# Gabor stage of a four-layer kernel: the way back over the rows for two channel groups at once, and the next group's rows forward placed ahead of it

## Chip, cores and metric

The kernel runs on one core of a Trainium2 chip. The metric is device time in microseconds, the median of three runs. A profile of one further execution is read beside it. The engines are called as the profile calls them: PE is TensorE's matmul and PEld its weight load, DVE is VectorE, ACT is ScalarE, POOL is GpSimd, and SP is SyncE, which issues the DMAs.

## The reference, cut to what matters

The program chains four layers over an image `x` of 4 x 64 x 128 x 128 float32: a Mamba layer, a Gabor layer, two convolutions with a gate, and a Mamba layer with a feed-forward part. The change touches the second layer, which computes, with `NUM, SIZE = 4, 32`:

```python
agray = x.reshape(B, a, b, C)                     # 4 x 128 x 128 x 64
rr, hh = analysis_window_r0(q, LEN, NUMBER)       # q from the image's gradients
S = rrb[d[:, :, None, None], d[None, None, :, :]]
ag = agray.reshape(B, num, size, num, size, C)
R1 = jnp.einsum('bikjlc,minjkl->bmnklc', ag.astype(jnp.complex64), S)
FT = jnp.fft.fft2(R1, axes=(3, 4))
xb = (FT.real - FT.imag).reshape(B, a, b, NB, bs)
o1 = jax.nn.relu(jnp.einsum('...bi,bio->...bo', xb, w1) + b1)
o2 = jnp.einsum('...bi,bio->...bo', o1, w2) + b2
xs = _softshrink(o2, LAMBD).reshape(B, num, num, size, size, C)
Rf = jnp.fft.fft2(xs, axes=(3, 4))
aa = Rf.real - Rf.imag
Gm = hh[ridx[:, :, None, None, :], ridx[None, None, :, :, :]]
I = jnp.einsum('bmnklc,xmynl->bxkylc', aa, Gm).reshape(B, a, b, C)
return I.reshape(B, C, a, b) + bias               # bias = x
```

So each image goes through a windowed transform over its rows and its columns, a small block-diagonal network over channels with a soft threshold, a transform back over columns and rows, and the image is added.

## The kernel before

`layer1` first computes the window (gradients over the whole image, then an iterative dual window), and builds constant matrices: `fa` and `fb` for the transforms forward over rows and columns, `ga` and `lt` for those back. Then it loops over the 4 images `b` and, in each, over 4 groups `g` of `G = 16` channels: 16 groups in all. An image is held in SBUF as `X`, with a row of the image in each partition and 128 columns by 64 channels in it. A group goes through six steps of TensorE, each of which writes PSUM tiles of 1024 elements a partition; all of them come from one ring of four (`ps`):

- Rows forward (L1041): for each channel, the weights are `X[:, :, c]` and the moving operand is `fa`, 256 columns. DVE copies the four tiles to `Z` (L1044), which has two buffers.
- Columns forward (L1052): weights from `Z`, moving operand `fb`, 128 columns. ACT copies two tiles to `O` (L1059).
- The network's first layer (L1065), 512 columns; ACT applies the relu into `O1` (L1066).
- Its second layer (L1072), 128 columns. DVE adds the bias into `xs` (L1073) and clamps it into `cl` (L1075), POOL subtracts the clamped part (L1076), which is the soft threshold. This is done in two halves, and `cl` has one buffer, so the second clamp waits for the first subtraction.
- Columns back (L1083): weights are one channel of `xs`, whose elements lie 16 floats apart; moving operand `ga`, 256 columns. ACT copies four tiles to `V` (L1086), laid out as `p i c (y l)`: real and imaginary part, channel, column.
- Rows back (L1094): for each of the 32 values of `l` two matmuls, for `i` 0 and 1, accumulate in PSUM. The weights are `lt[:, i, l]`, the moving operand is `Vl[:, i, l]`, 4 values of `y` by 16 channels, 64 columns. Channels lie 128 floats apart in it. DVE adds two tiles of 16 `l` each to `X` in place (L1101).

When an image's groups are done, SP stores `X` (L1102). `X` has two buffers and SP loads an image ahead (L1029).

The work is issued in the order in which the code states it, engine by engine, and each engine takes its own instructions in that order. Waits between engines are set by the tiles that they share. In the code below the way back of a group is therefore followed on TensorE by the rows forward of the next.

Of the kernel before, what the change touches and what calls it, by code (L numbers as in the profile page):

```python
# [10 lines left out]
F32 = mybir.dt.float32  # L11
# [6 lines left out]
P = 128  # L18
B, C, HH, WW = 4, 64, 128, 128
# [4 lines left out]
NUM, SIZE = 4, 32  # L24
# [7 lines left out]
G = 16  # L32
# [705 lines left out]
def _gradients(ctx, tc, K, x1, out):  # L738
# [9 lines left out]
    with tc.tile_pool(name="sob", bufs=2) as sp, tc.tile_pool(name="sobc", bufs=1) as sc, tc.tile_pool(  # L748
# [5 lines left out]
        for b in range(B):  # L754
            img = x1[b].rearrange("c (h r w) -> (c h) r w", h=2, w=C)
            for r0 in range(0, HH, R):
                X = sp.tile([P, R + 2, C], F32, name="X", tag="X")
                h = sp.tile([P, R + 2, C + 1], F32, name="h", tag="h")
# [205 lines left out]
@with_exitstack  # L964
def layer1(ctx, tc, K, w, x1, x2):
    nc = tc.nc
    cp = ctx.enter_context(tc.tile_pool(name="l1c", bufs=1))

    mg = cp.tile([P, 1], F32, name="mg")
    _gradients(ctx, tc, K, x1, mg)  # L970

    lm = cp.tile([P, 1], F32, name="lm")
    nc.scalar.activation(lm, mg, AF.Ln, scale=20.0 / (HH * WW))
    nscale = cp.tile([P, 1], F32, name="nscale")
    nc.scalar.activation(nscale, lm, AF.Exp, scale=0.5)
    nc.vector.tensor_scalar_mul(nscale, nscale, -math.pi / 25.0)
    amp = cp.tile([P, 1], F32, name="amp")
    nc.vector.tensor_scalar(amp, lm, 0.125, 0.25 * math.log(2.0) - 0.5 * math.log(5.0), ALU.mult, ALU.add)
    nc.scalar.activation(amp, amp, AF.Exp)
    r4 = cp.tile([P, NUM], F32, name="r4")  # L980
    _dual_window(tc, K, lm, nscale, r4)

    def outer(name, col_, tab):

        t = cp.tile([P, NUM, SIZE], F32, name=name)
        nc.vector.tensor_mul(
            t, tab.unsqueeze(1).to_broadcast([P, NUM, SIZE]), col_.unsqueeze(2).to_broadcast([P, NUM, SIZE])
        )
        return t


    fa = cp.tile([P, 2, NUM, SIZE], F32, name="fa")
    fb = cp.tile([P, 2, NUM, SIZE], F32, name="fb")
    rb = r4.unsqueeze(2).to_broadcast([P, NUM, SIZE])
    for t, i, tab in ((fa, 0, K.cos), (fa, 1, K.nsin), (fb, 0, K.cps), (fb, 1, K.smc)):
        nc.vector.tensor_mul(t[:, i], tab.unsqueeze(1).to_broadcast([P, NUM, SIZE]), rb)

    hm = cp.tile([P, NUM, SIZE], F32, name="hm")
    hmf = hm.rearrange("p y l -> p (y l)")
    nc.scalar.activation(hmf, K.dist, AF.Exp, scale=nscale)  # L1000
    nc.vector.tensor_scalar(hmf, hmf, amp, None, ALU.mult)
    ga = cp.tile([P, 2, NUM, SIZE], F32, name="ga")
    lt = cp.tile([P, 2, SIZE, NUM, SIZE], F32, name="lt")
    for i, tab, rtab in ((0, K.cps, K.cos), (1, K.cms, K.sin)):
        nc.vector.tensor_mul(ga[:, i], hm, tab.unsqueeze(1).to_broadcast([P, NUM, SIZE]))
        for xx in range(NUM):
            nc.vector.tensor_mul(
                lt[:, i, :, xx, :],
                hm[:, xx, :].unsqueeze(2).to_broadcast([P, SIZE, SIZE]),
                rtab.unsqueeze(1).to_broadcast([P, SIZE, SIZE]),  # L1010
            )

    NG = C // G
    w1 = cp.tile([P, NG, P], F32, name="w1")
    nc.sync.dma_start(w1, w["w1bd"].rearrange("g p q -> p g q"))
    w2 = cp.tile([P, NG, P], F32, name="w2")
    nc.sync.dma_start(w2, w["w2bd"].rearrange("g p q -> p g q"))
    b1 = cp.tile([P, NG], F32, name="b1")
    nc.sync.dma_start(b1, w["b1p"])
    b2 = cp.tile([P, NG, P], F32, name="b2")  # L1020
    nc.sync.dma_start(b2.rearrange("p g q -> p (g q)"), w["b2r"].to_broadcast([P, NG * P]))

    xp = ctx.enter_context(tc.tile_pool(name="l1x", bufs=2))
    wp = ctx.enter_context(tc.tile_pool(name="l1w", bufs=1))
    pa = ctx.enter_context(tc.tile_pool(name="l1p", bufs=4, space=PSUM))
    MU = P // G
    for b in range(B):
        X = xp.tile([P, HH, C], F32, name="X1", tag="X1")
        nc.sync.dma_start(X, x1[b].rearrange("c (h r w) -> (c h) r w", h=2, w=C))  # L1029
        for g in range(NG):  # L1030
            ch = slice(g * G, (g + 1) * G)

            def ps():
                return pa.tile([P, 1024], F32, name="p1", tag="p1")


            Z = wp.tile([P, 2, P, G], F32, name="Z", tag="Z", bufs=2)
            for c0 in range(0, G, 4):
                p = ps().rearrange("p (c i m) -> p c i m", c=4, i=2)
                for c in range(4):  # L1040
                    nc.tensor.matmul(  # L1041
                        p[:, c], X[:, :, g * G + c0 + c], fa.rearrange("p i m k -> p (i m k)"), start=True, stop=True
                    )
                nc.vector.tensor_copy(Z[:, :, :, c0 : c0 + 4].rearrange("p i m c -> p c i m"), p)  # L1044

            O = wp.tile([P, G, P], F32, name="O", tag="O")
            for k0 in range(0, G, 8):
                p = ps().rearrange("p (k n) -> p k n", k=8)
                for k in range(8):
                    rows = slice((k0 + k) * MU, (k0 + k + 1) * MU)  # L1050
                    for i in range(2):
                        nc.tensor.matmul(  # L1052
                            p[:, k],
                            Z[:, i, rows, :].rearrange("p m c -> p (m c)"),
                            fb[:, i].rearrange("p m k -> p (m k)"),
                            start=i == 0,
                            stop=i == 1,
                        )
                nc.scalar.copy(O[:, k0 : k0 + 8], p)  # L1059

            O1 = wp.tile([P, G, P], F32, name="O1", tag="O1")
            for k0 in range(0, G, 8):
                p = ps().rearrange("p (k n) -> p k n", k=8)
                for k in range(0, 8, 4):
                    nc.tensor.matmul(p[:, k : k + 4], w1[:, g], O[:, k0 + k : k0 + k + 4], start=True, stop=True)  # L1065
                nc.scalar.activation(O1[:, k0 : k0 + 8], p, AF.Relu, bias=b1[:, g : g + 1])  # L1066
            xs = wp.tile([P, G, P], F32, name="xs", tag="xs")
            for k0 in range(0, G, 8):
                ks = slice(k0, k0 + 8)
                p = ps().rearrange("p (k n) -> p k n", k=8)  # L1070
                for k in range(8):
                    nc.tensor.matmul(p[:, k], O1[:, k0 + k], w2[:, g], start=True, stop=True)  # L1072
                nc.vector.tensor_add(xs[:, ks], p, b2[:, g].unsqueeze(1).to_broadcast([P, 8, P]))  # L1073
                cl = wp.tile([P, 8, P], F32, name="cl", tag="cl")
                nc.vector.tensor_scalar(cl, xs[:, ks], -LAMBD, LAMBD, ALU.max, ALU.min)  # L1075
                nc.gpsimd.tensor_sub(xs[:, ks], xs[:, ks], cl)  # L1076

            V = wp.tile([P, 2, G, P], F32, name="V", tag="V", bufs=2)
            xr = xs.rearrange("p k (m c) -> p (k m) c", c=G)
            for c0 in range(0, G, 4):  # L1080
                p = ps().rearrange("p (c i m) -> p c i m", c=4, i=2)
                for c in range(4):
                    nc.tensor.matmul(  # L1083
                        p[:, c], xr[:, :, c0 + c], ga.rearrange("p i m k -> p (i m k)"), start=True, stop=True
                    )
                nc.scalar.copy(V[:, :, c0 : c0 + 4, :].rearrange("p i c m -> p c i m"), p)  # L1086

            Vl = V.rearrange("p i c (y l) -> p i l y c", l=SIZE)
            Xl = X[:, :, ch].rearrange("p (y l) c -> p l y c", l=SIZE)
            for l0 in range(0, SIZE, 16):  # L1090
                p = ps().rearrange("p (l y c) -> p l y c", l=16, y=NUM)
                for l in range(16):
                    for i in range(2):
                        nc.tensor.matmul(  # L1094
                            p[:, l],
                            lt[:, i, l0 + l].rearrange("p x k -> p (x k)"),
                            Vl[:, i, l0 + l],
                            start=i == 0,
                            stop=i == 1,
                        )  # L1100
                nc.vector.tensor_add(Xl[:, l0 : l0 + 16], Xl[:, l0 : l0 + 16], p)  # L1101
        nc.sync.dma_start(x2[b].rearrange("c (h r w) -> (c h) r w", h=2, w=C), X)  # L1102


# [522 lines left out]
```

## Time and profile before

| what | value |
|---|---|
| median of 3 runs | 19720.83 us (19693.8 to 19727.24) |
| the profiled execution's own time | 19736.35 us |
| its span, first to last instruction | 19734.5 us |
| mean granted TensorE clock over the span | 0.869 |
| the Gabor stage's loop | 4096 to 5006 us of the span |
| busy in it: PE, DVE, ACT, POOL | 752, 214, 133, 75 us |

The Gabor loop is 910 us of the span, 4.6%. The two Mamba stages ahead of it and after the convolutions take most of the rest. In the profile, a matmul of float32 operands is shown as two passes, each with its weight load, so that 64 matmuls appear as x128. The number before the engine is the start and the next the duration; the brackets at the end of a line of the timeline hold the time that the engine sat idle before it and what ended that.

### The profile page before, as it was taken

The numbers are of one execution on the slowest core, as the hardware profiler recorded it, in microseconds if no ns is written. First come the engines' busy times: TensorE is split into PE (matmuls) and PEld (weight loads), VectorE is DVE, ScalarE is ACT, GpSimd is POOL, SyncE is SP. The second block draws the span as 40 slices with busy tenths as digits, with TensorE's granted clock in tenths as the row PEclk, the third lists the DMA queues.
The fourth block names the chain that finished last, engine by engine and source line by source line (L and its number), as shares of the span: only waits on it lengthen the run. The fifth ranks groups of instructions, "written<-read, shape, count | busy, mean of one in ns | idle before, by whom it ended". The sixth has DMA issues, their size and how long they took to land. (4 is left out here: it accounts for less than half of the span.)

```text
span 19734.5 us, 238606 instructions
## 1 busy us (share of the span) xinstructions
PE 15294.8 (78%) x80186; PEld 7627.5 (39%) x80186; DVE 15836.0 (80%) x8739; ACT 14933.8 (76%) x30369; POOL 14205.9 (72%) x8094
## 2 busy tenths in 40 slices
PE   7778788778897777777777777777777777777777
PEld 3333333367434333333333333333333333333222
DVE  7888888722124999999999999999999999999755
ACT  7888888411324988889888888988889888888422
POOL 6888888500003898899988989998898988989300
PEclk8999899879998888888888888888888888888888
DMA  5555555300212232332323233232322323233111
GB/s 138 152 150 153 154 150 151 95 37 26 75 56 65 75 88 77 84 82 79 87 75 87 78 83 86 76 88 77 83 82 79 87 76 86 78 82 85 46 43 38
DMA packets 669524, 1722.89 MB, mean 87 GB/s; under 512 B 196785, under 2 KB 231937, under 8 KB 660865
## 3 DMA queue, kind: packets, MB, share of 16 engines
q1 hardware_dynamic: 668288, 1707.62, 31.6%
q8 instruction: 629, 10.31, 0.2%
q14 instruction: 607, 4.96, 0.1%
HBM read 1434.27 MB, written 272.63 MB: 86 GB/s over the span
## 5 line engine op out<-in xcount | busy, mean ns | idle before, releaser
L596 POOL TENSOR_TENSOR ring<-ring,cb 128x1024 f32<-128x1024 f32 x5120 | 12086.1, 2378 | 1653.5 <-DVE ring L593 1340.8
L593 DVE TENSOR_TENSOR_SCAN ring<-da,state,bx 128x1024 f32<-128x1024 f32 x4848 | 11143.4, 2335 | 971.1 <-PE bx L494 697.9
L556 ACT ACTIVATE da<-dl,A 128x1024 f32<-128x1024 f32 x5120 | 5868.2, 1146 | 1383.0 <-DVE ring L593 1365.9
L387 ACT ACTIVATE bxT<-duT,BT 128x128 f32<-128x128 f32 x21504 | 6757.2, 387 | 0.0
L494 PE MATMUL bx<-cst,bxT 128*128 128x128 f32 x24576 | 4458.7, 338 | 2842.8 <-DVE bx L587 2053.0
L494 PEld LDWEIGHTS bx<-cst,bxT 128*128 128x128 f32 x24576 | 3743.1, 214 | 4917.0 <-DVE bx L587 2068.7
L413 PE MATMUL y<-ring,cst 128*32 128x512 f32 x20480 | 3566.6, 660 | 332.4 <-POOL ring L596 332.2
L587 DVE TENSOR_TENSOR bx<-du,bx 128x1024 f32<-128x1024 f32 x2048 | 2515.5, 1228 | 339.6 <-PE bx L500 219.1
L413 PEld LDWEIGHTS y<-ring,cst 128*32 128x32 f32 x20480 | 532.3, 112 | 1735.7 <-POOL ring L596 856.1
L1145 PE MATMUL cv<-img,cw 64*64 64x512 f32 x9216 | 1008.2, 594 | 74.6 <-DMA img<-d_x 45.6
L500 PE MATMUL bx<-xc,spread 128*128 128x512 f32 x2048 | 1018.0, 620 | 1.4
L1427 POOL MEMSET h<- 128x18 f32 x64 | 8.3, 132 | 1180.5 <-PE pd L1489 793.5
L1076 POOL TENSOR_TENSOR xs<-xs,cl 128x1024 f32<-128x1024 f32 x32 | 74.9, 2340 | 1068.4 <-DVE cl L1075 1068.4
L391 POOL TENSOR_TENSOR bxT<-duT,BT 128x512 f32<-128x512 f32 x768 | 809.2, 1054 | 11.5 <-ACT duT L370 11.5
L1310 POOL MEMSET X<- 64x1 f32 x4 | 0.4, 89 | 1122.4 <-DMA cw<-in_l_conv_wT 1122.4
L1489 PE MATMUL pd<-h,diag 64*64 64x512 f32 x4608 | 687.9, 610 | 0.7 <-issue 0.7
L1145 PEld LDWEIGHTS cv<-img,cw 64*64 64x64 f32 x9216 | 437.2, 134 | 643.5 <-issue 568.0
L593 DVE TENSOR_TENSOR_SCAN ring<-da,bx 128x1024 f32<-128x1024 f32 x272 | 609.4, 2276 | 72.4 <-PE bx L494 52.8
L500 PEld LDWEIGHTS bx<-xc,spread 128*128 128x128 f32 x2048 | 347.7, 189 | 687.7 <-issue 464.1
L1461 DVE SCALAR_TENSOR_TENSOR g<-h,dww,g 128x2048 f32<-128x2048 f32 x256 | 602.0, 2352 | 11.2
L1441 ACT ACTIVATE h<-ph,ff_fc_b 128x384 f32<-128x384 f32 (+1 forms) x384 | 200.7, 577 | 497.9 <-PE ph L1436 480.1
L1059 ACT COPY O<-p 128x1024 f32<-128x1024 f32 x32 | 32.4, 1012 | 691.7 <-PE p L1052 691.7
(321 smaller groups left out, 13361.0 us busy)
## 6 DMA issues: line engine op xcount, KB each, us to landing
cb<-c SPq DMA_DIRECT2D x5120, 128.0 KB, 2.8
dl<-d SPq DMA_DIRECT2D x2048, 128.0 KB, 3.4
du<-d SPq DMA_DIRECT2D x2048, 128.0 KB, 3.0
d<-pos SPq DMA_DIRECT2D x128, 512.0 KB, 2.6
d<-u SPq DMA_DIRECT2D x128, 512.0 KB, 3.0
X<-d_t SPq DMA_DIRECT2D x124, 256.0 KB, 4.0
S<-in_x SPq DMA_DIRECT2D x120, 256.5 KB, 4.4
res<-in_x SPq DMA_DIRECT2D x128, 128.0 KB, 3.8
```

The lines of the kernel that those rows point to most:

```text
L387: nc.scalar.activation(t[:, k, q].rearrange("p e j -> p (e j)"), c["duT"][:, k, :], AF.Copy, scale=c["BT"][:, k, n : n + 1])
L391: nc.gpsimd.tensor_mul(t[:, k].rearrange("p q e j -> p q (e j)"), c["duT"][:, k].unsqueeze(1).to_broadcast(shape), c["BT"][:, k, NQ * g : ...
L413: nc.tensor.matmul(c["y"][DD * j : DD * (j + 1), _COLS[h]], K.sel, hc[:, _COLS[h]], start=False, stop=u["g"] == self.ng - 1,)
L494: nc.tensor.transpose(bx[:, P * k : P * (k + 1)], v["bxT"][:, k, :, :, j].rearrange("p q e -> p (q e)"), self.K.eye)
L500: nc.tensor.matmul(bx[:, k], self.spread[v["g"]], v["c"]["xc"][:, k], start=True, stop=True)
L556: nc.scalar.activation(das[nexp], v["c"]["dl"][k], AF.Exp, scale=self.A[:, k, v["g"] : v["g"] + 1])
L587: nc.vector.tensor_mul(bxs[i], u["c"]["du"][j], u["B"])
L593: nc.vector.tensor_tensor_scan(hs, das.pop(i), bxs.pop(i), 0.0 if u["c"].get("reset") else st, ALU.mult, ALU.add)
L596: nc.gpsimd.tensor_mul(hc, hs, u["cb"])
L1145: nc.tensor.matmul(p[i][half[h]], W[half[i], k, :], src[half[i], at : at + 4, dx : dx + WW], start=k == 0, stop=k == 8,)
L1461: nc.vector.scalar_tensor_tensor(g1, tap, wk, g1, ALU.mult, ALU.add)
L1489: nc.tensor.matmul(pd[i][half[h]], diag[half[i], k, :], h0[half[i], r : r + 4, dx : dx + WW], start=k == 0, stop=k == 8,)
```

## The change

It has two parts. The rows forward become a function, `transformed(b, g)`, which loads the image when `g` is 0, makes a group's `Z` and returns it. It is called once ahead of the loop for the first group; in the loop it is called for the next group (the next image's first group after the last of an image) between the soft threshold of this group and the columns back of this group.

And the way back over the rows is done for two groups together: `V` holds 32 channels in one buffer instead of 16 in each of two, an even group fills its first half and goes on to the next group, and an odd group fills the second half and then runs rows back over both. The moving operand has 4 x 32 = 128 columns, there are 64 matmuls for a pair of groups instead of 64 for each, and the sums are added to `X` in four tiles of 8 `l` for a pair.

```diff
+    def transformed(b, g):
+
+        if not g:
+            Xs[b] = xp.tile([P, HH, C], F32, name="X1", tag="X1")
+            nc.sync.dma_start(Xs[b], x1[b].rearrange("c (h r w) -> (c h) r w", h=2, w=C))
+        Z = wp.tile([P, 2, P, G], F32, name="Z", tag="Z", bufs=2)
+        for c0 in range(0, G, 4):
+            p = ps().rearrange("p (c i m) -> p c i m", c=4, i=2)
+            for c in range(4):
+                nc.tensor.matmul(
+                    p[:, c], Xs[b][:, :, g * G + c0 + c], fa.rearrange("p i m k -> p (i m k)"), start=True, stop=True
+                )
+            nc.vector.tensor_copy(Z[:, :, :, c0 : c0 + 4].rearrange("p i m c -> p c i m"), p)
+        return Z
+
+
+    Zn = transformed(0, 0)
     for b in range(B):
...
+        X = Xs[b]
         for g in range(NG):
...
+            Z = Zn
...
                 nc.gpsimd.tensor_sub(xs[:, ks], xs[:, ks], cl)
-
-            V = wp.tile([P, 2, G, P], F32, name="V", tag="V", bufs=2)
+            if (b, g) != (B - 1, NG - 1):
+                Zn = transformed(*divmod(b * NG + g + 1, NG))
+
+            if g % 2 == 0:
+                V = wp.tile([P, 2, 2 * G, P], F32, name="V", tag="V")
+            v0 = g % 2 * G
...
-                nc.scalar.copy(V[:, :, c0 : c0 + 4, :].rearrange("p i c m -> p c i m"), p)
+                nc.scalar.copy(V[:, :, v0 + c0 : v0 + c0 + 4, :].rearrange("p i c m -> p c i m"), p)
+            if g % 2 == 0:
+                continue
 
             Vl = V.rearrange("p i c (y l) -> p i l y c", l=SIZE)
-            Xl = X[:, :, ch].rearrange("p (y l) c -> p l y c", l=SIZE)
-            for l0 in range(0, SIZE, 16):
-                p = ps().rearrange("p (l y c) -> p l y c", l=16, y=NUM)
-                for l in range(16):
+            Xl = X[:, :, (g - 1) * G : (g + 1) * G].rearrange("p (y l) c -> p l y c", l=SIZE)
+            for l0 in range(0, SIZE, 8):
+                p = ps().rearrange("p (l y c) -> p l y c", l=8, y=NUM)
+                for l in range(8):
...
-                nc.vector.tensor_add(Xl[:, l0 : l0 + 16], Xl[:, l0 : l0 + 16], p)
+                nc.vector.tensor_add(Xl[:, l0 : l0 + 8], Xl[:, l0 : l0 + 8], p)
```

The other removed lines of the diff are the old place of the same code.

More of the change, by code (lines that the diff above doesn't have):

```diff
@@ L1026, in layer1, with ps @@
     MU = P // G
+    def ps():
+        return pa.tile([P, 1024], F32, name="p1", tag="p1")
+    Xs = {}
+    def transformed(b, g):
[12 more added lines that the diff above has]
+    Zn = transformed(0, 0)
     for b in range(B):
-        X = xp.tile([P, HH, C], F32, name="X1", tag="X1")
-        nc.sync.dma_start(X, x1[b].rearrange("c (h r w) -> (c h) r w", h=2, w=C))
+        X = Xs[b]
         for g in range(NG):
[L1031 to L1044, printed above, removed]
+            Z = Zn
             O = wp.tile([P, G, P], F32, name="O", tag="O")
```

## The prediction

> **What bounds the kernel now.** The edit touches the Gabor stage alone, 4096 to 5006 us of the 19734.5 us span. I read the stage's waits on TensorE, then one group in the timeline, then the stage's groups by form, then busy time and granted clock by stretch.
>
> TensorE's waits in the stage (engine, line, releaser: us in total, times, longest):
>
> ```profile
> PE p L1083 <- POOL xs L1076: 95.7, 16, 6.0
> PE p L1052 <- DVE Z L1044: 31.3, 16, 2.0
> PE p L1094 <- ACT V L1086: 17.6, 16, 1.1
> PE p L1041 <- DMA X<-d_x: 12.4, 1, 12.4
> ```
>
> No other engine comes near: in 910 us TensorE is busy 752, DVE 214, ACT 133, POOL 75. So the stage is TensorE's queue plus what it stands for: 16 groups of channels, each with the same three stalls. A steady group in the timeline (start, us; idle time before it in brackets):
>
> ```profile
> 4167.48 7.34 PE L1041 MATMUL p<-fa,X 128*128 128x256 f32 x32
> 4176.78 7.41 PE L1052 MATMUL p<-fb,Z 128*128 128x128 f32 x64 [1.96 <-DVE Z L1044]
> 4187.47 3.73 PE L1072 MATMUL p<-w,O 128*128 128x128 f32 x32
> ...
> 4194.79 2.34 POOL L1076 TENSOR_TENSOR xs<-xs,cl 128x1024 f32<-128x1024 f32 x1 [0.81 <-DVE cl L1075]
> 4197.18 9.76 PE L1083 MATMUL p<-ga,xs 128*128 128x256 f32 x32 [5.98 <-POOL xs L1076]
> ...
> 4208.05 14.54 PE L1094 MATMUL p<-V,lt 128*128 128x64 f32 x128 [1.10 <-ACT V L1086]
> ```
>
> Each fp32 matmul is two passes, so x128 are the 64 matmuls of the way back. L1041 and L1083 have one shape, yet take 7.34 and 9.76 us. The stretches 6 us before L1083, at its start and later (columns end in granted clock, DMA share, GB/s) show why:
>
> ```profile
> 4191.04:4197.18 6.14, 0.16 (x2) 0.00 (x0) 2.26 (x3) 0.00 (x0) 4.68 (x2) 0.85 0.00 0
> 4197.18:4201.00 3.82, 3.82 (x9) 3.07 (x10) 0.00 (x0) 0.00 (x0) 0.00 (x0) 0.50 0.02 4
> 4202.50:4206.90 4.40, 4.40 (x21) 4.15 (x19) 0.00 (x0) 2.03 (x2) 0.00 (x0) 1.00 0.00 0
> ```
>
> After the stall it starts at half clock. The stage's groups by form (busy us, mean ns) price the passes:
>
> ```profile
> L1094 PE MATMUL p<-V,lt 128*128 128x64 f32 x2048 | 232.6, 289 | 17.6 <-ACT V L1086 17.6
> L1083 PE MATMUL p<-ga,xs 128*128 128x256 f32 x512 | 152.3, 468 | 95.7 <-POOL xs L1076 95.7
> L1052 PE MATMUL p<-fb,Z 128*128 128x128 f32 x1024 | 138.1, 304 | 31.3 <-DVE Z L1044 31.3
> L1083 PEld LDWEIGHTS p<-ga,xs 128*128 128x128 f32 x512 | 132.7, 313 | 113.5 <-POOL xs L1076 98.8
> L1072 PE MATMUL p<-w,O 128*128 128x128 f32 x512 | 59.7, 275 | 0.0
> L1072 PEld LDWEIGHTS p<-w,O 128*128 128x128 f32 x512 | 59.6, 192 | 7.7 <-ACT O L1066 6.0 <-issue 0.2
> ```
>
> Pace from start to start, full clock: 64 columns (L1094) 0.1116 us, from the 7.14 us between the two adds of 64 passes; 128 columns (L1052) 0.110, from 3.52 us between its two evictions; 256 columns (L1041) 0.2213, from 1.77 us between evictions. So 64 columns cost as much as 128: the narrow matmul is bound by something else than its columns.
>
> [...] fp32 passes of 16 columns (L259, wbc) go at 0.113 us, so loading sets a floor that covers 64 columns. [...] The trace agrees after 5.98 us idle (0.50), and shows half clock in most L1052 after 1.96 us too (9.04 instead of 7.41 us). [...] Here the trace bears on the weights: L1083's are read 64 bytes apart and one load lasts 308 ns (median), L1072's contiguous ones 192. [...] The moving operand of L1094 is strided too: V[:, i, c, y, l] at fixed l steps 512 bytes from channel to channel. No row shows its rate by itself.
>
> **The change, part by part.** In the built TensorE order the forward rows of group g+1 (32 passes) stand between L1072 and L1083 of group g; the way back follows odd groups alone, in 32 pairs of 128 columns.
>
> (1) L1083's wait. POOL's second subtraction ends at 4197.13; the moved rows fill TensorE from 4191.04 to 4198.1. The wait goes in 15 of 16 groups (the last has nothing to move up): 95.7 - 6.0 = 89.7 us.
>
> (2) L1052's wait for Z: Z is ready a whole L1083 earlier, 31.3 - 2.0 = 29.3 us; only the first group keeps it.
>
> (3) V's wait (1.1 us) is met once per pair: 8 x 1.1 = 8.8.
>
> (4) Each break also lets the pipeline drain: consecutive lines overlap by about 0.17 us (L1065 ends at 4187.63, L1072 starts at 4187.47). 15 + 15 + 8 breaks: 6.4.
>
> (5) Half clock. L1083 is busy 152.3, at L1041's warm 7.34 it would be 117.4; 15/16 of the 34.9 is 32.7. L1052: 138.1 against 16 x 7.41 = 118.6, 15/16 of 19.5 is 18.3. The dense convolution stage at 5060 to 5160 us (busy 100 of 100 us) is granted 1.00, so a full queue is not throttled there.
>
> (6) The way back, 2048 passes now at 0.1116 = 228.5 us, becomes 1024 passes of 128 columns. Bounds: 0.1116 (reads are free, the load floor decides) gives 114.3; half-rate reads[...] with the overhead seen at 256 columns 0.2213, give 226.6. It cannot be above 2 x 0.1116, or 64 columns would not fit their own pace now, unless longer patterns read worse. I take 0.2213: saves 1.9. First passes speak the same way: after a stall L1094's first lasts 359 ns, L1052's with twice the columns 377[...].
>
> (7) At nothing: 8-row pieces make 4 adds of 1.22 us per pair, as many as before, and they end within a way-back piece of 3.5 to 7 us. The single V buffer is rewritten by the next pair's L1086 over 30 us after its last reader. SP's queue keeps its order (load 0, load 1, store 0, load 2, ...); no DMA is added. What is late next is DVE: Z's four copies (1.87 each) now queue behind the second clamp, which waits for POOL and ends at 4194.71. They end at 4196.6, 4198.4, 4200.3, 4202.2, and free the PSUM tiles that L1083's four pieces need at 4198.1, 4199.9, 4201.7, 4203.4: 1.2 us to spare, so nothing. Cover gone, L1083 would wait, and xs and V behind it.
>
> Sum: 89.7 + 29.3 + 8.8 + 6.4 + 32.7 + 18.3 + 1.9 = 187.1 us. The profiled execution took 19736.35 us (span 19734.5), 15.5 above the median; 187 off gives 19549, against the median 19720.83 it is **19534**. Layer 2 starts after the last add and store as before, so the gain reaches the end whole.
>
> **Rivals.** *The strided moving read is free, or nearly.* For: the pace of L1094 is also the load floor, so the trace does not show the read[...]. Against: the weights' 308 ns and the first pass. It saves 114.2 in (6): 299 in all, 19421; partial rates lie between.
>
> *The wait comes back as a wait for Z's copies.* For: only 1.2 us to spare, and DVE and POOL run side by side there. If each copy chain is held for one POOL subtraction (2.34), L1083 waits 1.1 us in 15 groups, 17; and if short gaps keep the clock low as they do at L1052, (5)'s 51 stays: 187 - 68 = 119, 19602. Against: the copy reads PSUM, and in the scan stages, where DVE is 9 tenths busy, POOL's 128x1024 product (L596) lasts 2378 ns against 2340 here (L1076): side by side costs them little.
>
> *Slower: the 128-column strided read is worse than twice the 64-column one*, since 32 channels span 16 KB of a partition instead of 8. It decides from the point where 1024 passes cost 228.5 + 185.2 (the rest of the sum) = 413.7, or 0.404 us a pass (3.2 ns a column); past the bound of the measurement at 0.443. At 0.5: 512 - 413.7 = 98 slower, 19819. Against: 64 columns fit in 0.1116, 1.74 ns a column, and nothing shows a longer pattern costing more.
>
> **How the numbers follow.** Half-rate read with the overlap working: 0.65, 19534, by itself 19510 to 19560. Free or partly free read: 0.25, 19421 to 19510. Copies in the way: 0.07. Slower: 0.03. The range 19410 to 19580 leaves out most of the third case, the fourth, and the edge of the second, as the runs shown spread by 33 us. This kernel can tell 0.2% (39 us) from no change. Faster 0.95, same 0.02, slower 0.03.
>
> **What the profile after would show.** L1083's wait for POOL left in one group (6.0 us) and L1052's in one (2.0); a granted clock of 1.00 across groups; forward rows, L1083 and L1052 at 7.3 us each; pairs of about 86 us, the stage near 710 us instead of 897 from first matmul to last add. Adds of the way back about 7.1 us apart confirm the half-rate read; 3.6 us apart show it free. I am wrong if TensorE waits for DVE's Z copies ahead of L1083, or if later stages change length by more than their 33 us of spread.

## The result, and the profile after

The changed kernel takes 19531.65 us (median of 4 runs, 19514.79 to 19542.05) against 19722.29 us for the kernel before (4 runs): a ratio of 0.9905, interval 0.9888 to 0.9923. The prediction was 19534 us in a range of 19410 to 19580.

In the code after, the lines of the loop have moved: rows forward is L1042, columns forward L1061, the second network layer L1081, the subtraction L1085, columns back L1096, the copy to V L1099, rows back L1109 and its add L1116. TensorE's waits in the stage, as before (line, releaser: us in total, times, longest):

```profile
PE p L1042 <- DMA X<-d_x: 12.3, 1, 12.3
PE p L1109 <- ACT V L1099: 8.8, 8, 1.1
PE p L1096 <- POOL xs L1085: 6.0, 1, 6.0
PE p L1061 <- DVE Z L1045: 2.0, 1, 2.0
```

POOL's wait is met once instead of 16 times, Z's once, V's 8 times. The timeline of a pair of groups shows a queue with one gap, ahead of the rows back:

```profile
4217.19 7.31 PE L1042 MATMUL p<-fa,X 128*128 128x256 f32 x32
4224.34 7.25 PE L1096 MATMUL p<-ga,xs 128*128 128x256 f32 x32
4231.43 7.31 PE L1061 MATMUL p<-fb,Z 128*128 128x128 f32 x64
...
4261.10 28.39 PE L1109 MATMUL p<-V,lt 128*128 128x128 f32 x128 [1.10 <-ACT V L1099]
```

Columns back now last 7.25 us instead of 9.76. The rows back of two groups last 28.4 us, and those of two groups before lasted 2 x 14.5: the pairing halved the passes and doubled their time. The stage's groups by form (busy us, mean ns, idle before):

```profile
L1109 PE MATMUL p<-V,lt 128*128 128x128 f32 x1024 | 227.1, 398 | 8.8 <-ACT V L1099 8.8
L1061 PE MATMUL p<-fb,Z 128*128 128x128 f32 x1024 | 118.8, 277 | 2.0 <-DVE Z L1045 2.0
L1096 PE MATMUL p<-ga,xs 128*128 128x256 f32 x512 | 118.5, 390 | 6.0 <-POOL xs L1085 6.0
```

From the first matmul of the stage to the start of its last add the loop took 897.1 us before and 705.6 after: 191.5 us of the 202.8 by which the two profiled executions differ. The other 11 lie outside of the stage, which the change does not touch, and within what varies there anyway: over the 13 profiled executions of this study, span less stage lies between 18792 and 18837 us, most of the variation in the second Mamba stage (12303 to 12347 us from the convolutions' last matmul to the first that writes `pd` in the feed-forward part). So below, the stage's length is what tells kernels apart by 10 us, and the run's time what it is worth.

### The profile page after: what moved, and what is told of

It is laid out like the page before. It is cut to its first block, busy times and chain, and to the rows that moved or that the text cites. A ratio compares the mean times of both kernels' runs of the same rounds, so it can differ in the third digit from the quotient of the medians.

```text
span 19531.8 us, 236579 instructions
## 1 busy us (share of the span) xinstructions
PE 15219.3 (78%) x79162; PEld 7559.7 (39%) x79162; DVE 15830.0 (81%) x8739; ACT 14931.3 (76%) x30369; POOL 14201.4 (73%) x8094
## 5 line engine op out<-in xcount | busy, mean ns | idle before, releaser
L1085 POOL TENSOR_TENSOR xs<-xs,cl 128x1024 f32<-128x1024 f32 x32 | 75.9, 2371 | 861.0 <-DVE cl L1084 861.0
L259 PE MATMUL pm<-S,cw 128*128 128x512 f32 x1024 | 521.3, 644 | 14.7 <-ACT sz L308 13.4
```

## Experiments

Each ratio is to runs of the kernel before that were taken beside that kernel (medians 19722 to 19727 us).

| kernel | stage, us | median, us | ratio to before (interval) |
|---|---|---|---|
| before | 897.1 | 19722 | |
| changed | 705.6 | 19531.65 | 0.9905 (0.9888 to 0.9923) |
| overlap alone | 784.5 | 19596.84 | 0.9932 (0.9918 to 0.9947) |
| pair alone | 878.9 | 19707.42 | 0.9988 (0.9979 to 0.9997) |
| pair, channels adjacent | 607.7 | 19409.35 | 0.9838 (0.9823 to 0.9853) |
| overlap, 64 columns, adjacent | 915.7 | 19743.06 | 1.0006 (0.9997 to 1.0014) |
| pair, two channels adjacent | 593.7 | 19408.56 | 0.9844 (0.9829 to 0.9858) |
| overlap alone, wait filled | 723.6 | 19556.77 | 0.9920 (0.9903 to 0.9936) |
| overlap, 64, adjacent, wait filled | 731.7 | 19558.56 | 0.9919 (0.9904 to 0.9934) |
| adjacent, columns forward early | 588.0 | 19411.99 | 0.9846 (0.9831 to 0.9861) |
| before, stall filled | 866.3 | 19691.15 | 0.9981 (0.9974 to 0.9988) |
| changed, late copies | 715.7 | 19533.80 | 0.9904 (0.9889 to 0.9919) |
| changed, spread copies | 726.4 | 19534.43 | 0.9910 (0.9893 to 0.9926) |

My theory was that the overlap carries the gain by taking away three waits and the half clock after them, and that the pairing gives almost nothing because its moving read is strided. The rivals: the pairing carries it; the pass is bound by its columns, not by its stride; the copies of Z become the new wait.

**Overlap alone.** Rows back once per group again, everything else as changed:

```diff
-            if g % 2 == 0:
-                V = wp.tile([P, 2, 2 * G, P], F32, name="V", tag="V")
-            v0 = g % 2 * G
+            V = wp.tile([P, 2, G, P], F32, name="V", tag="V", bufs=2)
...
-            if g % 2 == 0:
-                continue
```

> The rows forward of the next group stay ahead of the columns back, but the rows back run once per group again (64 columns, two buffers of V). If the pairing is worth almost nothing (strided reads at half rate), only its one missing wait for V is lost: 2048 passes at 0.1116 us = 228.5 against 225 measured in the changed kernel, 8 more waits of 1.1 us and 8 drains of 0.17: 14 us more, 19545 us; the adds of the rows back stay 7.1 us apart. If the pairing carries the gain (rival), the time goes back by over 100 us, to 19630 or more.

Measured 19596.84, 65 us above the changed kernel and 52 above what I expected. The waits are as expected (17.6 us for V, 16 times); the surprise is in the rows back. Three groups in the timeline:

```profile
4370.52 14.54 PE L1105 MATMUL p<-V,lt 128*128 128x64 f32 x128 [1.10 <-ACT V L1097]
...
4414.57 26.05 PE L1105 MATMUL p<-V,lt 128*128 128x64 f32 x128 [1.10 <-ACT V L1097]
...
4528.73 14.54 PE L1105 MATMUL p<-V,lt 128*128 128x64 f32 x128 [1.10 <-ACT V L1097]
```

The same 128 passes after the same wait take 14.5 or 26 us. Five of 16 groups are slow, 56 us in all (rows back busy 288.4 against 232.6 before), and the columns forward behind them lose 8 more (127.2 against 118.8). This is the count of one execution, 16 us above the median of the four; the others may have had fewer slow groups. In the slow group of 4414.57 us the granted clock falls to half at 4416.28, 1.71 us after its start, though TensorE has no gap there; the group of 4370.52 keeps the full clock. Two stretches of each (columns end in granted clock, DMA share, GB/s), between the times at which the clock changed or could have by the grid of 3.413 us that is measured further down:

```profile
4412.87:4416.28 3.41, 2.31 (x18) 2.01 (x18) 0.00 (x0) 1.01 (x1) 0.00 (x0) 1.00 0.00 0
4416.28:4419.69 3.41, 3.41 (x18) 3.41 (x18) 0.00 (x0) 0.00 (x0) 0.00 (x0) 0.50 0.00 0
...
4368.50:4371.91 3.41, 2.31 (x17) 2.01 (x16) 0.00 (x0) 1.21 (x2) 0.00 (x0) 1.00 0.00 0
4371.91:4375.33 3.42, 3.42 (x33) 3.42 (x33) 0.00 (x0) 0.00 (x0) 0.00 (x0) 1.00 0.02 5
```

**Pair alone.** Rows back in pairs, rows forward at the start of their own group:

```diff
-            if (b, g) != (B - 1, NG - 1):
-                Zn = transformed(*divmod(b * NG + g + 1, NG))
...
-            Z = Zn
+            Z = transformed(b, g)
```

> The rows back run for two groups at once, but each group's rows forward stand at its own start, as before. If the overlap carries the gain: TensorE waits again 16 times for POOL ahead of the columns back (95 us) and 16 times for Z (31 us), the columns back are busy about 150 us again at half clock, and the time is 19722 - 14 = 19708 us, which can't be told from the kernel before. If the pairing carried it (rival): 19610 us or less.

As expected: 19707.42, the waits for POOL and Z back at 96.0 and 31.3 us, columns back busy 154.7. The stage is 18.2 us shorter than before. The overlap alone saves 112.6, both together 191.5: 61 us belong to neither part alone (44 by the medians of the runs). They are about the 64 us of half clock that the overlap alone met; the paired rows back lose nothing to it, as is shown below.

**Pair, channels adjacent.** The channel is made V's innermost index:

```diff
-                V = wp.tile([P, 2, 2 * G, P], F32, name="V", tag="V")
+                V = wp.tile([P, 2, P, 2 * G], F32, name="V", tag="V")
...
-                nc.scalar.copy(V[:, :, v0 + c0 : v0 + c0 + 4, :].rearrange("p i c m -> p c i m"), p)
+                nc.scalar.copy(V[:, :, :, v0 + c0 : v0 + c0 + 4].rearrange("p i m c -> p c i m"), p)
...
-            Vl = V.rearrange("p i c (y l) -> p i l y c", l=SIZE)
+            Vl = V.rearrange("p i (y l) c -> p i l y c", l=SIZE)
```

> The changed kernel with V laid out with the channel innermost, so that the 32 channels of a moving read lie side by side; ScalarE's copy into V then writes one float in 32. If the stride is what holds the 128-column pass at 0.22 us: passes fall to the load floor of 0.11 us, 225 - 114 = 111 us less, 19421 us; the adds of the rows back come 3.6 us apart; ScalarE's copy may take longer than its 1.01 us (up to 1.8 us is hidden by TensorE's pace of 1.77 us per piece, and the last one lengthens the wait for V by the difference, under 10 us in all). If the pass is bound by its columns or by PSUM (rival): 19532 us as without it, adds 7.0 us apart.

The stride was the cause: the rows back are busy 123.0 us instead of 227.1, and the run takes 19409.35. In the groups by form, rows back and ScalarE's copy:

```profile
L1109 PE MATMUL p<-V,lt 128*128 128x128 f32 x1024 | 123.0, 285 | 15.6 <-ACT V L1099 15.6
...
L1099 ACT COPY V<-p 128x1024 f32<-128x1024 f32 x64 | 115.2, 1918 | 183.5 <-PE p L1096 183.5
```

The copy that writes one float in 32 lasts 1.9 us instead of 1.01. TensorE's pace hides all but the last, and V's wait grows from 8.8 to 15.6 us.

**Two channels adjacent.** Pairs of channels lie side by side, `V = [P, 2, G, P, 2]`, copied in two instructions for each piece.

> The changed kernel with V laid out so that two channels lie side by side (8 bytes) and the next pair 1024 bytes on; ScalarE copies each piece in two instructions. [...] the paired pass is at the load floor of 0.11 us, as with all 32 channels side by side: about 19415 us, adds 3.6 us apart. If each jump costs a fixed time (rival), a pass of 128 columns has 64 jumps instead of 128: between, about 0.17 us a pass or 19480 us.[...]

Two floats side by side are enough: 1024 passes of 128 columns in 116.5 us, the pace of the 64-column passes (2048 in 232.6), and ScalarE's two copies keep V's wait at 9.6 us:

```profile
L1112 PE MATMUL p<-V,lt 128*128 128x128 f32 x1024 | 116.5, 273 | 9.6 <-ACT V L1100 9.6
```

Single floats, 512 bytes apart, cost 0.2197 us per 128 columns (7.03 us between adds of 32 passes), floats in pairs, 8 bytes together, 0.112 (3.58). What makes two enough is not shown by these runs.

**64 columns, channels adjacent.** The overlap alone with the adjacent layout:

> The kernel of the overlap alone (rows back once per group, 64 columns) with V's channels innermost. If the load of the weights sets the floor at 64 columns, the layout changes nothing there: 19545 us as with the overlap alone, plus up to 10 us if ScalarE's copy is slower. If a strided read is dearer even at 64 columns (rival): some 50 to 100 us less than the overlap alone.

Neither came: 19743.06, no faster than the kernel before. ScalarE's slower copy made the wait for V longer, 1.96 us instead of 1.10, and half clock is the rule, in 14 of 16 groups:

```profile
4207.47 25.54 PE L1105 MATMUL p<-V,lt 128*128 128x64 f32 x128 [1.96 <-ACT V L1097]
...
4497.07 14.51 PE L1105 MATMUL p<-V,lt 128*128 128x64 f32 x128 [1.95 <-ACT V L1097]
```

Two groups that stayed at full clock took 14.5 us, as with the strided layout. So at full clock the stride costs nothing at 64 columns; what differs is how often the clock falls.

**The wait filled.** What lets the clock fall with a full queue: narrow matmuls by themselves, or the short wait ahead of them? In both 64-column kernels matmuls whose result nobody reads were put into the wait, 4 in the strided kernel and 5 in the adjacent one:

```diff
+            p = ps()
+            for k in range(4):
+                nc.tensor.matmul(p[:, :256], w2[:, g], fa.rearrange("p i m k -> p (i m k)"), start=True, stop=True)
             Vl = V.rearrange("p i c (y l) -> p i l y c", l=SIZE)
```

> The kernel of the overlap alone (64 columns), with 4 matmuls of 256 columns added ahead of the rows back of every group, whose result nobody reads: they fill the 1.1 us wait for V. In the profile of the overlap alone, 5 of 16 rows back ran at half clock (26 us instead of 14.5) with TensorE's queue full. If it is the short wait together with narrow matmuls that lets the clock fall, none falls now: 288 us of rows back become 233, the columns forward after them 127 to 119, and the added matmuls cost 16 x 0.5 us more than the wait: 19597 - 64 + 8 = 19541 to 19555 us. If 64 columns by themselves let it fall (rival): still several rows back of 26 us, about 19605 us.

> The kernel of overlap, 64 columns and adjacent channels, with 5 matmuls of 256 columns added ahead of the rows back, whose result nobody reads: they fill its wait for V of 1.96 us. There 14 of 16 rows back ran at half clock. If the wait sets it off: all rows back take 14.5 us, 375 - 232 = 143 us less, columns forward 29 us less: about 19575 us. If narrow matmuls that leave half of the array's time unused let the clock fall by themselves (rival): as without the filler, 19745 us.

All 32 rows back run at full clock, so the narrow matmuls alone don't do it: it takes the wait as well. (The 375 us in the second expectation should have been 386: the profile has those rows back busy for 385.8.) First the strided, then the adjacent kernel:

```profile
L1108 PE MATMUL p<-V,lt 128*128 128x64 f32 x2048 | 230.9, 288 | 0.0
```

```profile
L1108 PE MATMUL p<-V,lt 128*128 128x64 f32 x2048 | 232.0, 275 | 0.0
```

Adding useless work made these kernels 61 and 184 us shorter in the stage, 40 and 185 in the median. In the changed kernel the clock falls as well, for 3.41 us in three of the eight rows back, and it does no harm there: all eight last 28.4 us. Two stretches of one of them:

```profile
4176.95:4180.37 3.42, 3.42 (x17) 3.42 (x16) 0.00 (x0) 0.00 (x0) 0.00 (x0) 0.50 0.00 0
4180.37:4183.78 3.41, 3.41 (x17) 3.21 (x17) 1.22 (x1) 0.00 (x0) 0.00 (x0) 1.00 0.00 0
```

There are 17 passes in each, at clock 0.50 and at 1.00: the strided read sets their pace, not the clock. It is a close thing. Where passes of 128 adjacent columns fell to half clock (pair, channels adjacent), they came 0.2136 us apart, just under the 0.2197 of the strided read.

**The stall before, filled.** The kernel before with 12 matmuls of 256 columns in the 6 us stall:

```diff
+            p = ps()
+            for k in range(12):
+                nc.tensor.matmul(p[:, :256], w2[:, g], fa.rearrange("p i m k -> p (i m k)"), start=True, stop=True)
             V = wp.tile([P, 2, G, P], F32, name="V", tag="V", bufs=2)
```

> The kernel before, with 12 matmuls of 256 columns (24 passes, 5.3 us), whose result nobody reads, in the 6 us stall ahead of the columns back. Nothing is moved or paired. If the half clock after the stall comes from the idle time, the columns back fall from 152 us busy to about 118 and the wait for POOL from 95.7 us to about 11 (the filler takes it): stage 897 - 34 = 863 us, the run about 33 us faster. If the columns back are slow for another reason (fresh xs, strided weights; rival), they stay at 150 us and the run at 19722.

Measured 866.3 us in the stage and 19691.15. The columns back are at full clock, here those of one group, where the kernel before showed 0.50 after the stall:

```profile
4189.70:4197.17 7.47, 7.47 (x32) 7.17 (x32) 0.00 (x0) 3.04 (x3) 0.00 (x0) 1.00 0.00 0
...
L1087 PE MATMUL p<-ga,xs 128*128 128x256 f32 x512 | 119.4, 392 | 13.1 <-POOL xs L1076 13.1
```

The filler's 85.5 us only take the place of 82.6 us of waiting, so the 31 us that the stage is shorter come from the clock of the columns back, with nothing moved and nothing paired.

**Late copies.** Is it Z's copies that would be late next? Six clamps were added to VectorE behind the soft threshold:

```diff
+            for _ in range(6):
+                nc.vector.tensor_scalar(O[:, :8], O1[:, :8], -LAMBD, LAMBD, ALU.max, ALU.min)
             if (b, g) != (B - 1, NG - 1):
```

> The changed kernel with 6 more clamps of 128x1024 on VectorE, whose result nobody reads, between the soft threshold and the copies of Z: 6 x 0.69 = 4.2 us later for each copy. If the copies have about 1.8 us to spare, as the trace of the changed kernel shows for the last piece (copy ends 4227.87, piece starts 4229.65), the columns back wait 2.4 us in 15 groups: 36 us, stage 706 + 36 = 742 us, the run at 19567. If they were not what frees the pieces (rival): 19532.

This run doesn't answer. Four of the six clamps were sorted in ahead of the bias adds and two among them, not where the text has them (the order of an engine is the framework's, where data allow, and not only the code's as I wrote above), so the subtraction came late instead: columns back waited 0.2 us a group for POOL. A second form, with adds that read `cl`, can't move ahead:

```diff
+            for _ in range(6):
+                nc.vector.tensor_add(O[:, :8], cl, cl)
             if (b, g) != (B - 1, NG - 1):
```

> The changed kernel with 6 adds of 128x1024 on VectorE that read cl and whose result nobody reads; in the built order one stands after each of the first three copies of Z, the rest after the fourth. At 1.22 us each they make the second, third and fourth copy 1.2, 2.4 and 3.7 us later. In the changed kernel the last copy ended 1.8 us before its piece. If the copies free the pieces of the columns back, these wait 2 to 3 us in 15 groups: stage 706 + 33 to 45 = 739 to 751 us, the run at 19565 to 19577. If the copies are not what frees them (rival): stage 706, run 19532.

```profile
PE p L1098 <- DVE Z L1045: 10.5, 15, 0.7
```

The wait appears, 15 times, between the second and third piece: in all 15 groups the second and third piece start 0.05 to 0.06 us after the second and third copy end, so the mechanism of that rival is real. Its price is less than expected, 20.8 us in the stage: 10.5 as a wait, and 10.5 in columns back that are busy 129.0 us instead of 118.5. The expectation counted on the last copy, but the fourth piece starts 0.8 us before the fourth copy ends: it doesn't wait for it. The run's median doesn't show it (19534.43): it is hidden in the variation of the Mamba stages.

**Adjacent channels, columns forward early.** The next group's columns forward also go ahead of the rows back:

```diff
+            if (b, g) != (B - 1, NG - 1):
+                On = columns(Zn)
             if g % 2 == 0:
                 continue
```

> The paired kernel with adjacent channels, and the next group's columns forward moved ahead of the rows back as well, so that they cover the wait for V. That wait was 15.6 us in the profile (8 of 2.0 us), with drains of 0.17: if no new wait comes, 19409 - 15 = 19394 us. If ScalarE's copies of O, now behind those of V, hold the next step (rival): 19409 us.

V's wait is left once, in the last group (2.0 us), and the stage is the shortest, 588.0 us, 19.7 below the paired kernel with adjacent channels. The runs can't tell these two and two channels adjacent apart (19411.99, 19409.35 and 19408.56). The smallest change is channels adjacent: three lines, 122 us below the changed kernel.

## Why the prediction was right, point by point

- (1) to (3), the waits: 89.7, 29.3 and 8.8 us were to go; the waits in the profile went down by just these. No new wait came.
- (4), drains: not measured by themselves. What the other terms leave of the stage's 191.5 us is about 5, against 6.4.
- (5), half clock: columns back from 152.3 to 118.5 busy, 33.8 against 32.7; columns forward from 138.1 to 118.8, 19.3 against 18.3. The filled stall shows the first alone.
- (6), the way back: 0.2197 us a pass against 0.2213; busy time falls by 5.5 us against 1.9. That the strided read goes at half rate was an estimate, from weight loads of 308 ns against 192; the adjacent layouts show that the stride was the reason, which was the choice that decided between 19534 and 19421.
- (7), Z's copies: nothing, with 1.3 to 1.8 us to spare at every piece where I had 1.2.
- Sum: 187.1 predicted, 191.5 in the stage.
- The mark "granted clock of 1.00 across groups" was wrong in places: it fell to half in three of the eight rows back, without cost.

What the sum hid is the worth of the parts. By my terms the overlap alone would have saved 175 us and the pairing 12. Measured: 112.6 and 18.2, and 61 more only together. I had taken the pace of the 64-column passes from a kernel in which all 16 rows back stayed at full clock, after the same 1.1 us wait. That they may fall once the rest is moved stood in no term. The end was right because the strided passes of the pair take 0.22 us at half clock as at full. That too stood in no term, so on this point the prediction was lucky.

Why did all 16 stay at full clock in the kernel before and 11 of 16 in the overlap alone, after the same wait? In each of the 13 profiles, all changes of the granted clock within the stage lie whole multiples of 3.413 us apart, to within 3 ns. So each profile has a grid of steps of 3.413 us, and the waits can be sorted by where in a step they lie. Seven of the profiles (the kernel before, the changed one, overlap alone, pair alone, stall filled and the two with late copies) have the 1.10 us wait for V, 80 times together. The clock fell 13 times, and each time the step in which the rows back started had begun 0.68 to 1.79 us ahead of them: it held most of the wait and 1.6 to 2.7 us of rows back. The other 67 times, all 16 of the kernel before among them, it had begun at most 0.21 or at least 1.86 us ahead. By this sorting the kernel before was spared by where its waits lay, and moving the rows forward moved the waits.

The wait and its place are not all. With two channels adjacent, a wait of 1.20 us lay in that range 4 times, and the passes that followed, of twice as many columns in the same time, kept the full clock.

What stays open: all this is sorted from what happened; no run sets the position by itself, and what makes the clock change on such a grid, and why the waits of the kernel before all lay outside of the range, is not shown.

## What to carry to other kernels

Find out what binds a matmul before making it wider. Here a float32 pass took 0.43 us for 512 columns and 0.2213 for 256, but 0.110 to 0.113 for 128, 64 and 16 alike, and 0.2197 for 128 columns read one float at a time. That the load of the weights sets the 0.11 us is my estimate, from the equal pace and from PEld, which is busy 229.9 of the 232.6 us of the rows back before. Going from 64 to 128 columns halved the rows back only with two floats side by side (232.6 to 116.5 us) or all 32 (123.0); with single floats it left 227.1. Where a wait of 1 to 2 us stands ahead of narrow matmuls, a profile in which the clock holds is no promise: after the same 1.10 us it fell 0 times of 16 in the kernel before and 5 of 16 in the overlap alone. Look at the granted clock there again after every change; filling the wait kept the clock up 32 times of 32. And where a kernel varies by 40 us elsewhere, judge a stage by its own length in the profile.

## What the runs showed of the hardware that was not expected

- TensorE's clock fell to half with its queue full: in 64-column passes, which cost as much as 128 columns (0.112 us), after a wait of 1.10 us (5 of 16 times in the overlap alone, 0 of 16 in the kernel before) or 1.96 us (14 of 16). It then stayed down for 27.3 us, into the columns forward, where these followed; with the wait filled, 0 of 32. With 128 adjacent columns after 1.96 us, 4 of the 8 rows back took 16.2 us instead of 14.56: it fell and came back after 3.41 us.
- With one and the same wait of 1.10 us, what told falls from no falls was its place in the grid of 3.413 us on which the clock changed: 13 falls in the 13 cases in which the step had begun 0.68 to 1.79 us ahead of the passes, none in the 67 elsewhere.
- A strided float32 moving read keeps 0.22 us per 128 columns at clock 0.50 as at 1.00; 128 adjacent columns take 0.112 at full and 0.2136 at half clock.
- In the two kernels with late copies, VectorE's add of two SBUF operands beside POOL's subtraction lasted 1.88 us against 1.20 alone, and its clamp 2.03 against 0.69, while the copies out of PSUM kept 1.9 us: which form is beside POOL matters.
